# Post-norm decoder layer on one core: tokens transposed by VectorE in 32x32 blocks and regrouped by way of DRAM in place of TensorE's transposes, with self-attention in three streams

## Chip, cores and metric

The kernel runs on one core of a Trainium2 chip, in float32. The metric is the device time of one execution in microseconds (us): the median of several runs. Profiles show one execution; PE is TensorE's matmul, PEld its weight load, DVE is VectorE, ACT is ScalarE, POOL is GpSimd, and SP is SyncE, whose queue (SPq) issues the DMA transfers. L12 means line 12 of the kernel.

## What is computed

One decoder layer over 16 batches of 512 tokens with 256 channels (B = 16, S = 512, C = 256). The reference, cut to its core:

```python
# 1. linear attention: 16 heads of 16 channels, K = 2 states, multiplied
q  = x + x @ Wq + bq
ks = x + x @ Wk[k] + bk[k];  vs = x + x @ Wv[k] + bv[k]        # k = 0, 1
state = prod_k (ks_h.T @ vs_h) / 1024                           # per head, over the 512 tokens
o  = layernorm(q_h @ state) * ln_g + ln_b;  o = o @ Wo + bo
x  = layernorm(x + o)
# 2. cross-attention to 64 context tokens per batch, 16 heads of 64
x  = layernorm(x + softmax(q k.T / 8) v @ Wout.T + b_out)
# 3. 8 experts of 256 -> 1024 -> 256; softmax router; each expert takes
#    the first 1024 tokens whose weight is above 0
x  = layernorm(x + combined expert outputs)
```

## The kernel before

**Tiles.** A batch is NT = 4 tiles of 128 tokens (tokens on partitions, channels along the free axis) and NC = 2 halves of 128 channels. Eight router columns are carried beside the 256 channels, so many tiles are CX = 264 wide. With these inputs the experts take the first two batches (HEAD_B = 2); a loop at the end of the program serves further batches if their tokens have capacity left.

**Work of one batch.** `gram` (L544) multiplies x by itself (ps_g). `self_attention` (L608) loads x again (`load_x`, L603, tile xt), makes the two states (ps_gk L623, ps_s L635), transposes x (`transposed`, L227, into xT), folds the state and Wq into one matrix (ps_m, ps_b), multiplies xT by it (ps_o, L681), normalizes the result z (L687), transposes z (L694) while ScalarE applies gain and shift on the way out of PSUM (zT, L695), multiplies by Wo (ps_p, L705), adds x, normalizes (x1, L713), and transposes x1 (L717) into x1T. A 257th channel row of ones is written into x1T for the mask: VectorE's operation at L237 does it with `not_last`. `cross_attention` (L759) multiplies x1T by keys folded into Wq (ps_sim, L808), makes the softmax (maximum and difference on VectorE, exponential on ScalarE, a product on GpSimd, a 32x32-block transpose on VectorE, L798), and multiplies 128 times with 32 rows each (ps_x, L828). `routing` (L840) normalizes and makes the expert weights. `experts` (L923) is one long run of ps_h (L940) and ps_e (L957) matmuls that has no part in the batches after the first two.

**TensorE's transposes.** `transposed` writes eight 128x128 transposes, four to a PSUM bank; ScalarE and VectorE copy the two banks out. For xT, zT and x1T that is 24 transposes a batch, 384 in all. The weights and the context use the same helper at the start.

**What sets the order.** The parts are Python generators, each in a `Stream` (grams, context, self, cross, routing, experts) with a planned start and span. `weave` (L1004) always resumes the ready stream whose planned time is earliest; `yield` gives up the turn, `yield WAIT` keeps the stream out until the planner's `Model` (L28, durations by engine and size) thinks that its operations are done. `in_order` (L1023) then pins the recorded order on TensorE, VectorE, ScalarE and GpSimd. Nothing is reordered on the chip: an engine that reaches an instruction whose input is late waits, and everything behind it waits too. DMA transfers are all issued by SP in its own order.

**Buffers.** Pool wk1 has one buffer for each name: xt, z, and xT (shared by xT and zT). Pool wk2 has two (x1, x1T, s) and six for the context tiles vo. PSUM has eight banks for everything.

## Time and profile before

| | |
|---|---|
| median of three runs | 1392.32 us (1389.68 to 1394.6) |
| the profiled execution's own time | 1391.12 us |
| its span in the profile | 1389.4 us |
| granted TensorE clock | 0.995 |
| VectorE, ScalarE, GpSimd busy | 850.5, 402.2, 203.9 us |
| DMA moved | 153.57 MB, mean 111 GB/s |
| first ps_x block starts, last one ends | 190.6 us, 1340.4 us |

The profiled execution's time lies 1.7 us above its span and 1.2 us below the median. The page shows busy time by engine, then the span in 40 slices, the DMA queues, the chain of work that ended last, and groups of instructions. A group's mean time is the length of one instruction, but TensorE's instructions overlap; how long one holds the engine is read from the starts in the timeline. TensorE shows two records for each float32 matmul and one for each transpose.

### The profile page before, as it was taken

What the parts mean: (1) busy time and instruction counts of PE and PEld (TensorE: products, weight loads), DVE (VectorE), ACT (ScalarE), POOL (GpSimd) and SP (SyncE); (2) the same over time, 40 slices, a digit from 0 to 9 for tenths busy, and PEclk for the clock granted to TensorE, in tenths of its full rate; (3) what the DMA queues carried; (4) which work ended last, traced back from release to release, by engine and by line L of the source; (5) the groups of instructions that cost most, each with busy time, mean ns of one, the idle gap of its engine ahead of it and who ended that gap; (6) DMA issues with size and microseconds to landing.
All of it is one profiled execution on the core that took longest, in us unless ns stands there. A gap on an engine that the chain in (4) does not pass through costs nothing.

```text
span 1389.4 us, 24206 instructions
## 1 busy us (share of the span) xinstructions
PE 1363.8 (98%) x9630; PEld 1075.8 (77%) x9630; DVE 850.5 (61%) x1957; ACT 402.2 (29%) x912; POOL 203.9 (15%) x140
## 2 busy tenths in 40 slices
PE   7999999999999999999999999999999999999997
PEld 4666676877878787878878787878888787878686
DVE  2345848466583848476584848475675939484744
ACT  1134323132232314142233223142323323232322
POOL 0001112112020111112020112112020202111200
PEclk9999999999999999999999999999999999999999
DMA  8657775511516153421606053513334061505211
GB/s 261 202 121 193 201 188 169 141 32 33 154 46 157 46 141 106 123 80 47 186 18 169 31 141 106 126 62 75 112 94 124 16 187 46 147 26 126 91 55 40
DMA packets 98373, 153.57 MB, mean 111 GB/s; under 512 B 15561, under 2 KB 70097, under 8 KB 98257
## 3 DMA queue, kind: packets, MB, share of 16 engines
q1 hardware_dynamic: 98256, 151.98, 39.9%
q8 instruction: 78, 1.28, 0.4%
q14 instruction: 39, 0.31, 0.1%
HBM read 114.71 MB, written 37.22 MB: 109 GB/s over the span
## 4 chain that ended last, share of the span: by engine, by line
PE 90%; DVE 6%; DMA 2%; ACT 1%; issue 0%; SPq 0%; DVEq 0%; ACTq 0%
PE ps_x L828 17%; PE ps_sim L808 15%; PE ps_e L957 15%; PE ps_h L940 14%; PE ps_p L705 4%; PE ps_gk L623 4%; PE ps_o L681 3%; PE ps_kv L436 3%; PE ps_t L233 2%; PE ps_vo L486 2%; PE ps_kq L745 2%; PE ps_s L635 2%; PE ps_g L549 2%; PE ps_zt L694 1%; PE ps_m L664 1%; PE ps_g L554 1%
## 5 line engine op out<-in xcount | busy, mean ns | idle before, releaser
L940 PE MATMUL ps_h<-head_T,wi 128*128 128x256 f32 x1024 | 239.1, 379 | 0.0
L828 PE MATMUL ps_x<-vo,pT 32*128 32x264 f32 x4096 | 234.4, 385 | 3.7 <-DVE pT L798 3.7
L808 PE MATMUL ps_sim<-kq,x1T 128*128 128x512 f32 x512 | 235.0, 593 | 0.0
L828 PEld LDWEIGHTS ps_x<-vo,pT 32*128 32x128 f32 x4096 | 212.5, 186 | 24.5 <-issue 5.6
L940 PEld LDWEIGHTS ps_h<-head_T,wi 128*128 128x128 f32 x1024 | 193.4, 190 | 38.8 <-issue 13.0
L796 POOL TENSOR_TENSOR s<-s,sm 128x1024 f32<-128x1024 f32 x64 | 121.8, 1903 | 539.1 <-DVE sm L795 500.7
L835 DVE TENSOR_TENSOR x<-ps_x,x 128x264 f32<-128x264 f32 x64 | 23.2, 426 | 225.6 <-PE ps_x L828 225.6
L816 ACT ACTIVATE s<-s 128x512 f32<-128x512 f32 x128 | 80.7, 630 | 276.0 <-DVE s L815 276.0
L808 PEld LDWEIGHTS ps_sim<-kq,x1T 128*128 128x128 f32 x512 | 94.5, 190 | 83.2 <-issue 74.2
L814 DVE TENSOR_REDUCE mx<-ps_sim 128x8 f32<-128x512 f32 x128 | 86.1, 672 | 42.2 <-PE ps_sim L808 41.9
L815 DVE TENSOR_TENSOR s<-ps_sim,mx 128x512 f32<-128x512 f32 x128 | 88.5, 692 | 4.4
L719 POOL TENSOR_TENSOR x<-x,bout 128x1056 f32<-128x1056 f32 x16 | 38.8, 2422 | 320.9 <-ACT hT L946 172.6
L798 DVE STREAM_TRANSPOSE pT<-s 128x1024 f32<-128x1024 f32 x64 | 78.6, 1228 | 7.0 <-POOL s L796 7.0
L946 ACT ACTIVATE hT<-ps_h 128x256 f32<-128x256 f32 x128 | 47.0, 377 | 119.9 <-PE ps_h L940 119.7
L695 ACT ACTIVATE zT<-ps_zt,shift,gain 128x512 f32<-128x512 f32 x32 | 23.2, 776 | 189.7 <-PE ps_zt L694 189.7
L794 DVE TENSOR_REDUCE sm<-s 128x16 f32<-128x1024 f32 x64 | 77.1, 1204 | 0.4 <-ACT s L816 0.4
L267 ACT ACTIVATE x<-x,off,rstd 128x264 f32<-128x264 f32 (+1 forms) x112 | 58.3, 591 | 29.3 <-DVE off L265 29.3
L681 PE MATMUL ps_o<-m,xT 128*128 128x264 f32 x256 | 66.7, 387 | 0.0
L261 ACT ACTIVATE rstd<-bn_mv,eps 128x4 f32<-128x4 f32 (+1 forms) x70 | 20.7, 295 | 158.6 <-DVE bn_mv L250 155.1
L948 DVE TENSOR_SCALAR hT<-ps_h 128x256 f32<-128x256 f32 x128 | 52.1, 409 | 22.5 <-PE ps_h L940 22.3
L705 PE MATMUL ps_p<-wo,zT 128*128 128x264 f32 x256 | 63.1, 387 | 0.0
L436 PE MATMUL ps_kv<-cT,wT 128*128 128x512 f32 x128 | 61.1, 612 | 0.2 <-ACT vst L186 0.2
(172 smaller groups left out, 1892.6 us busy)
## 6 DMA issues: line engine op xcount, KB each, us to landing
vo<-vo_dram SPq DMA_DIRECT2D x512, 132.0 KB, 4.1
vo_dram<-vst SPq DMA_DIRECT2D x128, 132.0 KB, 2.4
xt<-in_x_dram SPq DMA_DIRECT2D x16, 512.0 KB, 4.0
wi<-L_ffn_experts_inter_dram SPq DMA_DIRECT2D x8, 1024.0 KB, 5.1
gx<-in_x_dram SPq DMA_DIRECT2D x15, 512.0 KB, 4.2
x_rest<-x SPq DMA_DIRECT2D x14, 512.0 KB, 3.0
out_dram<-x SPq DMA_DIRECT2D x14, 512.0 KB, 2.9
k_dram<-st SPq DMA_DIRECT2D x16, 256.0 KB, 3.5
```

The source lines that it names most:

```text
L436: nc.tensor.matmul(ps, wT[:, cc, r % 4 * P:(r % 4 + 1) * P], cT[:, cc, q * 512:(q + 1) * 512], start=(cc == 0), stop=(cc == NC - 1),)
L681: nc.tensor.matmul(ps[:, :CX], xT[:, cc, t * P:(t + 1) * P], m[:, cc, :], start=(cc == 0), stop=(cc == NC - 1))
L705: nc.tensor.matmul(ps[:, :CX], zT[:, cc, t * P:(t + 1) * P], wo[:, cc, :], start=(cc == 0), stop=(cc == NC - 1))
L796: nc.gpsimd.tensor_mul(s, s, sm.unsqueeze(2).to_broadcast([P, NH, J]))
L798: nc.vector.transpose(probsT[:, :, t, :], s.rearrange("p h (a j) -> p (h a) j", a=2))
L808: nc.tensor.matmul(ps, x1T[:, cc, t * P:(t + 1) * P], kq[:, cc, hf * 512:(hf + 1) * 512], start=(cc == 0), stop=(cc == NC - 1),)
L814: nc.vector.tensor_reduce(mx[:, hs], sim, AX.X, ALU.max)
L815: nc.vector.tensor_sub(s[:, hs, :], sim, mx[:, hs].unsqueeze(2).to_broadcast([P, 8, J]))
L816: nc.scalar.activation(s[:, hs, :], s[:, hs, :], AF.Exp, scale=SCALE)
L828: nc.tensor.matmul(ps[q][:, :CX], probsT[pq, blk].rearrange("p t i -> p (t i)"), vos[c][pq, i, :], start=(c == 0 and i == 0), stop=(c == 7 ...
L940: nc.tensor.matmul(ps[:, :TB], wi[:, cc, f * P:(f + 1) * P], head_T[b][:, cc, t0 * P:t0 * P + TB], start=(cc == 0), stop=(cc == NC - 1),)
L957: nc.tensor.matmul(ps[:, :C], hT[f][:, t * P:(t + 1) * P], wo_[:, f, :], start=(f == 0), stop=(f == NF - 1),)
```

## The change

The three token transposes of a batch leave TensorE. `to_blocks` lets VectorE transpose each of the four token tiles in 32x32 blocks into one tile xb. `put` writes xb to DRAM with one transfer from ScalarE's queue, and `regroup` reads it back with four transfers of 32 partitions each, in runs of 256 floats, so that channels come to lie on partitions (xT by SP; zT and x1T by ScalarE's queue). xb is a single buffer, and `taken` keeps a second user out until the transfer to DRAM is issued. The transposed tiles now lie as [channel, token tile, half, token], so the matmuls index them as `xT[:, t, cc]`.

For x the blocks are made in `gram`, from gx, and stay in DRAM until `self_attention` loads them; the next gx is loaded after that. Gain and shift, which rode on zT's copy, are folded into Wo and its bias once, at the start: two matmuls and a few VectorE operations in `router_weights`. The ones of x1T are written by ScalarE on a part of x1's blocks (`last_q`). The router columns of z move into xt in 16 small GpSimd copies a batch in place of one.

The states become a stream of their own (`self_states`, `all_states`), and what follows the second normalization (`scores_operand`) another. `yield LIGHT` is a wait after which the stream may be resumed ahead of others, since it issues no TensorE work; `yield HOLD` lets only such streams come between the eight parts of the ps_x block, which stays in one piece on TensorE. The planner takes 0.35 us of ScalarE and 3.0 us to landing for a transfer on ScalarE's queue. Instruction counts, from the order of the two programs: 384 transposes fewer and 2 matmuls more on TensorE; 192 block transposes on VectorE; 176 DMA issues on ScalarE and 64 more on SP.

```diff
+LIGHT = "light"
+HOLD = "hold"
...
+            if kind == "InstDMACopy" and engine == "Activation":
+                start = max(at, self.free.get(engine, 0.0))
+                self.free[engine] = start + 0.35
+                done = start + 3.0
...
+    taken = []
+    def to_blocks(src):
+        while taken:
+            yield LIGHT, 0.5
+        xb = wk1.tile([P, NT, NC, NT, 32], FP, tag="xb", name="xb")
+        for t in range(NT):
+            nc.vector.transpose(
+                xb[:, :, :, t, :].rearrange("p k c j -> p c k j"),
+                src[:, t, :C].rearrange("p (c k j) -> p c k j", c=NC, j=32),
+            )
+        taken.append(xb)
+        yield LIGHT
+        return xb
+    def blocks_dram(name):
+        return dram.tile([NT, 32, NT, NC * NT * 32], FP, tag=name, name=name)
+    def regroup(pool_, tag, name, there, eng):
+        dst = pool_.tile([P, NT, NC, P], FP, tag=tag, name=name)
+        for k in range(NT):
+            eng.dma_start(
+                out=dst[k * 32:(k + 1) * 32].rearrange("i q c n -> i q (c n)"),
+                in_=there[:, :, k, :].rearrange("q i n -> i q n"),
+            )
+        return dst
+    def put(there, xb):
+        nc.scalar.dma_start(
+            out=there.rearrange("q i k n -> (q i) (k n)"), in_=xb.rearrange("p k c t j -> p (k c t j)")
+        )
+        taken.clear()
...
@@ router_columns, router_weights
+            yield WAIT
             ps = bank("ps_rw")
...
+            for dc in range(NC):
+                nc.tensor.matmul(
+                    ps[:, :CX], shift_cols[:, dc, :], wo[:, dc, :], start=(dc == 0), stop=(dc == NC - 1)
+                )
+            nc.vector.tensor_add(cs["bo"], ps[:, :C], cs["bo"])
+            nc.vector.tensor_add(bq_state[:, C:], ps[:, C:CX], bq_state[:, C:])
+            for dc in range(NC):
+                nc.vector.tensor_scalar(wo[:, dc, :], wo[:, dc, :], cs["gain"][:, dc:dc + 1], None, ALU.mult)
...
@@ gram
-            if b + 2 < B:
-                gram_x[b + 2] = load_gram_x(b + 2)
...
+            xb = yield from to_blocks(gx)
+            x_blocks[b] = blocks_dram(f"x_blocks{b}")
+            put(x_blocks[b], xb)
+            if b + 2 < B:
+                gram_x[b + 2] = load_gram_x(b + 2)
...
@@ self_states (was the head of self_attention)
+            yield from until(lambda: finished["self"] >= b, LIGHT)
             state = wk1.tile([P, NC, P], FP, tag="state", name="state")
...
-            yield from until(lambda: made(xt))
-            transposed(xT, xt)
-            yield WAIT
+        def self_attention(b, done):
+            xt = load_x(b)
+            xT = regroup(wk1, "xT", "xT", x_blocks.pop(b), nc.sync)
+            yield from until(lambda: b in states and made(states[b]))
...
-            zT = wk1.tile([P, NC, S], FP, tag="xT", name="zT")
-            for cc in range(NC):
-                ps = bank("ps_zt")
-                for t in range(NT):
-                    nc.tensor.transpose(ps[:, t * P:(t + 1) * P], z[:, t, cc * P:(cc + 1) * P], ident)
-                nc.scalar.activation(
-                    zT[:, cc, :], ps, AF.Identity, bias=cs["shift"][:, cc:cc + 1], scale=cs["gain"][:, cc:cc + 1]
-                )
-            nc.gpsimd.tensor_copy(xt[:, :, C:], z[:, :, C:])
+            for t in range(NT):
+                for q in range(NT):
+                    nc.gpsimd.tensor_copy(xt[q * 32:(q + 1) * 32, t, C:], z[t * 32:(t + 1) * 32, q, C:])
+            zb = yield from to_blocks(z)
+            z_blocks = blocks_dram(f"z_blocks{b % 2}")
+            put(z_blocks, zb)
...
+            yield from until(lambda: made(z_blocks), LIGHT)
+            zT = regroup(wk1, "xT", "zT", z_blocks, nc.scalar)
+            yield
+            yield from until(lambda: made(zT))
...
+            beside(self_st, scores_operand(b, xt, mm))
+        def scores_operand(b, xt, mm):
...
-            transposed(x1T, x1, lambda t: t.rearrange("p (t q i) -> p q t i", q=NT, t=NT), ones=True)
-            yield WAIT
+            x1b = yield from to_blocks(x1)
+            nc.scalar.activation(
+                x1b[:, NT - 1, NC - 1], x1b[:, NT - 1, NC - 1], AF.Identity, bias=last_q[:, 0:1], scale=last_q[:, 1:2]
+            )
+            x1_blocks = blocks_dram(f"x1_blocks{b % 2}")
+            put(x1_blocks, x1b)
+            yield LIGHT, 0.0
+            yield from until(lambda: made(x1_blocks), LIGHT)
+            x1T = regroup(wk2, "x1T", "x1T", x1_blocks, nc.scalar)
+            yield
+            yield from until(lambda: made(x1T))
...
@@ cross_attention, the ps_x block
                 if c < 2:
                     load_vo()
+                if c < 7:
+                    yield HOLD
...
@@ weave
-                st = min(now, key=Stream.time)
+                now = [st for st in now if st.light] or ([held] if held else now)
```

## The prediction

> **What bounds the kernel now.** I read the page's busy line first, then busy time by stage, then the timeline of TensorE around one transpose, then the transfers.
>
> ```profile
> PE 1363.8 (98%) x9630; PEld 1075.8 (77%) x9630; DVE 850.5 (61%) x1957; ACT 402.2 (29%) x912; POOL 203.9 (15%) x140
> PE 90%; DVE 6%; DMA 2%; ACT 1%; issue 0%; SPq 0%; DVEq 0%; ACTq 0%
> ```
>
> TensorE is busy all the time and 90% of the chain that ended last is its own work. Whether that holds in every stage is told by the same count in five stretches (length, then busy time of PE, PEld, DVE, ACT, POOL, clock, DMA share, GB/s): a stretch between two ps_x blocks, a ps_x block, and the start, middle and end of the run.
>
> ```profile
> 665.00:726.00 61.00, 60.87 (x289) 47.78 (x289) 46.65 (x111) 19.05 (x44) 11.96 (x8) 1.00 0.32 95
> 726.00:740.40 14.40, 14.40 (x257) 12.97 (x257) 0.67 (x1) 2.07 (x4) 0.65 (x1) 1.00 0.80 192
> 0.00:190.60 190.60, 178.30 (x881) 115.38 (x881) 96.78 (x227) 58.58 (x134) 17.57 (x27) 0.98 0.70 191
> 190.60:1340.40 1149.80, 1145.10 (x8573) 926.52 (x8572) 727.89 (x1645) 328.29 (x737) 186.35 (x113) 1.00 0.37 100
> 1340.40:1389.40 49.00, 40.41 (x181) 33.88 (x180) 25.81 (x85) 15.38 (x42) 0.00 (x0) 0.97 0.13 42
> ```
>
> In the 1150 us between the first and the last ps_x block TensorE is idle for 4.7 us. The other 20.9 us of idle time lie in the start (12.3) and the tail (8.6). So in the middle every microsecond of TensorE's work taken away is a microsecond gained, as long as no new wait comes. The clock there is 1.00, so there is no throttle to gain from or lose to.
>
> **What a transpose costs.** Its record says 273 ns, but records overlap. The starts in TensorE's timeline tell what eight of them hold:
>
> ```profile
> 699.40 1.04 PE L233 MATMUL ps_t<-ident,xt 128*128 128x128 f32 x8
> 700.27 1.03 PE L940 MATMUL ps_h<-head_T,wi 128*128 128x256 f32 x4
> ...
> 754.43 1.04 PE L233 MATMUL ps_t<-ident,x 128*128 128x128 f32 x8
> 755.30 1.89 PE L957 MATMUL ps_e<-wo__5835,hT 128*128 128x256 f32 x8
> ```
>
> Each group of eight delays the next work by 0.87 us; the zT group, from 740.40 to 741.33, by 0.93. Three groups in 16 batches: 32 x 0.87 + 16 x 0.93 = 42.7 us. Added on TensorE are two 264-wide matmuls at 0.45 us each (ps_p's, 747.50 to 748.39 for two): 0.9 us. **TensorE's work falls by 41.8 us.**
>
> [...]
>
> **What VectorE and ScalarE pay.** VectorE gets 192 block transposes of 256 elements. Before has only the four times larger one:
>
> ```profile
> L798 DVE STREAM_TRANSPOSE pT<-s 128x1024 f32<-128x1024 f32 x64 | 78.6, 1228 | 7.0 <-POOL s L796 7.0
> ```
>
> A quarter of 1228 ns is 0.31 us, the lower end; a 512-element VectorE pass (L815) takes 0.69, the upper end. I take 0.35, near the quarter because the time of the larger one follows its length: 67 us (59 to 133). The copies of xT and x1T leave VectorE: 16 x (0.683 + 0.810) = 24 us. Net 43 us, or 2.7 a batch. Between two ps_x blocks VectorE is 46.65 of 61 us busy, 76%; with all of it there and 2.6 us less TensorE work, 49.3 of 58.4, 84%. In the ps_x block it is idle but for 0.67 us, and the light streams may use that. I cost it at nothing, covered by this idle time. ScalarE loses 32 x 0.776 + 9.4 + 9.2 = 43 us and gains 16 copies of 128 elements (0.25 each, 4 us) and 176 DMA issues. An issue on SP takes 0.39 us (xt's row, below); on ScalarE none is shown. I bound it by nothing and by 0.63, one of its exponentials (L816), and take SP's 0.39: 69 us. ScalarE is at 29%: hidden, except that each issue holds evacuations behind it, four in a row for 1.6 us, in which TensorE fills about four of eight banks (ps_h, 0.43 us a bank).
>
> **What the path of a token tile pays.** This is what can cost time: TensorE's order is fixed, so a late xT, zT or x1T stops it. The nearest rows are the loads of xt (512 KB, runs of 1024 bytes, like a regrouping), the first fence, and the stores of x2_rest (512 KB, like a put), the second. The SPq row has min, median and max of one issue in ns.
>
> ```profile
> L605 SPq DMA_DIRECT2D xt<-in_x_dram x16: 389/390/556, 38.3 to 1208.0; - x16
> ...
> DMA to landing us min/median/max: 3.8/4.0/5.7
> ```
>
> ```profile
> L864 SPq DMA_DIRECT2D x_rest<-x x14: 383/384/400, 376.7 to 1347.4; - x14
> ...
> DMA to landing us min/median/max: 2.8/3.0/4.5
> ```
>
> From the last ps_o to a loaded zT: sum, statistics and normalization of one tile 2.55 us (in the tail of the timeline, 1379.54 to 1382.09), three more tiles 1.5, four block transposes 1.4, the put 0.4 + 3.0, four issues 1.2 and the last landing 4.0: **14 us**; x1T has the same and a copy of 0.25. With the maxima it is 17.5. I counted the TensorE work between the two ends in the changed kernel's order, with the issue times of before's timeline (0.86 us for a 512-wide matmul, 0.43 for 256, 14.45 for a ps_x block). From last ps_o to first ps_p it is 19.2 us at the least in 16 batches, with a median near 28; from last ps_p to first ps_sim 19.1 at the least, with a median near 28. In the order of before the smallest are 10.5 and 7.2. So all 32 paths have 1.6 us or more over the slow sum.
>
> xT has its blocks in DRAM long before, but shares its buffer with zT, so its load waits for the last ps_p of the batch before. There the next ps_o follows after 3.2 us in the third batch, then 7.4 or more in all others. The load needs 1.2 + 4.0 = 5.2: **2 us** lost once. SP waits for that buffer too, and vo, xt and weight transfers stand behind it; the same happens before with xt, also a single buffer, and vo is needed some 60 us later.
>
> DMA moves 48 x 0.52 MB out and as much in: 153.6 MB become 204, and its share of 40% grows by bytes to about 53%. It is at 0.80 during ps_x, where the vo loads of the next batch run, so puts and loads that fall there come near their maxima, which the covers still hold.
>
> GpSimd's 16 small copies a batch, at 0.21 us each by the one copy that they replace (L698), and the sum behind them (2.36, L699) take 5.7 us and must end before the first ps_p's sum; they run beside the 10 us of put and load, and cost 0, or at worst the 3.2 us by which they grew if a softmax product (1.9 us) stands ahead.
>
> The DMA semaphores and single buffers add waits that no row shows: ScalarE now waits for puts before it issues loads. In the order a regrouping often stands directly behind its put, so ScalarE stands for some 3 us. Between nothing (it has nothing else ready) and 1 us for each of 32, I take 4 us in all, near the lower end since ps_x or VectorE's evacuations cover most of them.
>
> The start: a wait of 3.3 us (ps_rw for VectorE, L376) is given its own place in the plan; the two for pT ahead of ps_x, 3.7 together, are unchanged. Against it, gx is reloaded later, after its block transposes. I take these as equal, between 4 us less and 10 more, as idle time in the start is 12.3.
>
> **Sum.** 1389.4 - 41.8 + 2 + 4 = 1353.6 span; with the 1.7 us outside the span **1355 us**, 2.7% below the median of 1392.3 and 36 below the profiled execution's 1391.1. Taken without any new wait it is 1351, with 4 us less at the start 1347.
>
> **Rivals.**
>
> Better packing (0.18): the longer covers also take away waits that busy time hides in the start, where ps_g takes 0.41 us a record against 0.22 in the middle. With some 10 us of them gone it is 1340 to 1347. For it: 20.9 of 25.6 us idle lie outside the middle. Against: the start waits for input transfers.
>
> VectorE becomes the bound (0.17): at 84% between ps_x blocks its queue runs late, and TensorE waits for banks. At 1 to 2 us in each of 16 batches it gives 1365 to 1385. For it: 0.69 us for a transpose would add 5.5 us a batch, not 2.7. Against: ps_x leaves 13.7 us idle.
>
> Transfers eat the gain (0.08), slower than before: put and load behind the vo burst. If the path takes 26 us instead of 14, the sum of what is missing over the 32 counted covers is 39 us, so the gain is gone; at 28 it is 64 and the run takes 1355 + 64 = 1419 us. For it: a vo load of only 132 KB lands in 4.1 us in the median (page, DMA issues), so there is a backlog in the burst. Against it: 26 us need each of the two landings near 9 to 10 us, and the maxima shown are 4.5 and 5.7.
>
> That the change does not take the work off TensorE is excluded: the order has 384 transposes fewer.
>
> **How the numbers follow.** Forecast 0.55 (1347 to 1362), better packing 0.18, VectorE 0.17, transfers 0.08, and 0.02 near no change. The range takes in the first three but the ends: 1340 to 1380, leaving out 0.08 + 0.02 and some of the tails. A difference of 0.3%, 4 us, is about what a measurement of this kernel can tell. Faster 0.89 (the first three, less the far end of the third), same 0.03, slower 0.08.
>
> **What will show it.** ps_t and ps_zt rows gone except for weights, context and the head (106 transposes left); TensorE busy near 1322 us; idle in the middle under 15 us. Block transposes near 0.35 us each. Waits of ps_o, ps_p and ps_sim for transfers a few us in all; if they hold over 20 us, the covers were misjudged. If waits for VectorE after ps_sim or ps_h hold 20 us, the second rival is right. ScalarE's DMA issues at 0.4 us; if they take 1 us or more, ScalarE holds the banks and the forecast falls.

## The result and the profile after

The changed kernel takes **1462.88 us** (median of four runs, 1459.41 to 1467.07) against 1392.29 for the kernel before on the same chip: ratio 1.0509, 95% interval 1.047 to 1.0548. It is slower by 71 us where 37 us less than this median were forecast. The profiled execution has a span of 1457.7 us and a mean granted clock of 0.969 (before 1389.4 and 0.995). Further down, one of e3's four executions took 3585 us and is left out of its median.

The page of the changed kernel, busy time, then busy tenths of TensorE, its granted clock and DMA in 40 slices, then the chain that ended last:

```profile
PE 1363.8 (94%) x9250; PEld 1054.4 (72%) x9250; DVE 880.0 (60%) x2123; ACT 369.2 (25%) x864; POOL 247.9 (17%) x380
...
PE   7797998799899999999999999999999998999897
...
PEclk9899999899999999999999999999999999999999
DMA  8717869533451717463364527352727264533521
...
PE 56%; DVE 20%; DMA 7%; ACT 3%; issue 2%; SPq 1%; ACTq 0%; POOL 0%; DVEq 0%; POOLq 0%
```

TensorE has 380 instructions less and the same busy time, and its own work is 56% of the chain instead of 90%. The missing digits lie in the first third. Three of the prediction's stretches (up to the first ps_x, from there to the last one's end, the tail; length, then busy time of PE, PEld, DVE, ACT, POOL, clock, DMA share, GB/s) are now:

```profile
0.00:223.10 223.10, 192.99 (x883) 125.22 (x883) 108.21 (x270) 55.59 (x128) 23.10 (x56) 0.92 0.68 189
223.10:1404.80 1181.70, 1125.47 (x8165) 890.73 (x8164) 744.05 (x1764) 297.17 (x690) 224.76 (x324) 0.98 0.49 135
1404.80:1457.70 52.90, 45.32 (x204) 38.50 (x204) 27.76 (x90) 16.47 (x46) 0.00 (x0) 0.96 0.11 39
```

The start became 32.5 us longer, and the middle, which should have lost some 40 us of work, is 32 us longer. Idle time in the middle is 56.2 us (before 4.7). What TensorE waited for (us in total, times, longest):

```profile
PE ps_sim L880 <- DMA x1T<-x_blocks: 13.9, 3, 5.5
PE ps_rw L416 <- DVE early L412: 9.1, 1, 9.1
PE ps_o L739 <- DMA xT<-x_blocks: 8.5, 2, 6.3
PE ps_vo L535 <- ACT vst L193: 7.1, 6, 6.1
PE ps_s L684 <- DVE gk L673: 6.8, 1, 6.8
PE ps_e L1034 <- DVE hT L1025: 5.8, 4, 3.8
```

No single row explains the 109 us that are accounted for below; there are few waits for the transposed tiles themselves and many for VectorE and ScalarE.

**Why idle time is only part of it.** TensorE's timeline around the longest wait for x1T (start, length, operation), then three neighbouring stretches around the same place:

```profile
432.53 1.89 PE L1017 MATMUL ps_h<-head_T,wi 128*128 128x256 f32 x8
439.91 8.88 PE L880 MATMUL ps_sim<-kq,x1T 128*128 128x512 f32 x16 [5.49 <-DMA x1T<-x_blocks]
448.63 1.03 PE L1017 MATMUL ps_h<-head_T,wi 128*128 128x256 f32 x4
```

```profile
429.00:436.70 7.70, 5.42 (x25) 4.39 (x24) 4.85 (x17) 2.84 (x7) 0.00 (x0) 1.00 0.73 235
436.70:443.50 6.80, 3.59 (x5) 1.55 (x6) 0.00 (x0) 0.00 (x0) 0.00 (x0) 0.50 0.51 123
443.50:450.00 6.50, 6.50 (x20) 3.46 (x19) 5.28 (x8) 1.89 (x3) 0.00 (x0) 1.00 0.00 0
```

Sixteen ps_sim records take 8.72 us up to the next start, where eight products at 0.86 need 6.9: for 6.8 us the granted clock is 0.50, 3.2 of them still within the stall. So the stall of 5.5 us cost 1.8 us more in slow work. The changed kernel has 16 such half-clock stretches, 91.2 us together, the kernel before four, 15.4 us. TensorE was busy in 62.8 and 10.2 us of them; half of the difference, **26 us**, is lost work time. It is most of why busy time did not fall by 41 us. The account of the span: work 41 us less, idle time 68 more (93.9 against 25.6), half clock 26 more, 15 not assigned (perhaps short gaps that the records' overlap hides): 68 us more.

**The path of one tile.** The chain of waits from 425 to 442 us in the changed kernel (start, length, what):

```profile
425.37 5.67 DMA x_blocks<-xb
431.04 0.02 issue
431.06 0.32 ACTq L267
...
432.52 7.26 DMA x1T<-x_blocks
439.78 0.14 issue
439.91 2.90 PE ps_sim L880 x3
```

From the put to the loaded x1T are 14.4 us, where the prediction took 8.6 (11.8 with the maxima). In that time a store of 512 KB (x_rest, issued 424.72) and a load of 1024 KB (wo_, issued 430.97) are under way, and the DMA engines are busy for 0.90 of the put and 0.99 of the load (the last but one figure of each line):

```profile
425.40:431.00 5.60, 5.60 (x28) 4.88 (x27) 4.80 (x19) 0.73 (x3) 0.28 (x1) 1.00 0.90 323
432.50:439.80 7.30, 1.92 (x9) 1.33 (x8) 1.52 (x5) 2.34 (x5) 0.00 (x0) 0.79 0.99 274
```

A single piece of x1T lands in 3.1 us in the median, 7.4 at worst, but a tile needs its put and the last of four pieces. Where the trace tells all these landings, the way from the put's issue to the loaded tile takes 12.8 us in the median for x1T (6 batches, 7.3 to 14.1) and 10.8 for zT (7 batches, 7.1 to 11.9). So the 8.6 us were too little in general, and not in one bad place alone.

What stands ahead of the put grew more. From the last ps_p to the put of x1 the prediction counted 5.7 us (sum, statistics, normalization, block transposes, copy); the changed kernel's trace has 10.6 at the least and 15.0 in the median of the 16 batches. In the kernel before, the last ps_p to the first transpose of x1 took 5.0 to 8.9 us. The whole way of x1, from the last ps_p to the loaded tile, is 21.5 to 42.2 us in those 6 batches, 24.6 in the median, where the prediction has 14 (17.5 with the maxima). Some of this is the planner's choice, which may place other work ahead where the cover is long; how much is not shown.

**A common measure.** To compare kernels whose orders differ, every TensorE instruction is priced by its issue time in the kernel before, as in the prediction (0.86 us for a 512-wide product, 0.43 for 256, 0.87 for eight transposes, so 0.109 for one), and the sum in program order is taken from the start of the same instruction in the trace. What is left is time lost to waits and half clock up to there. In us:

| kernel | TensorE work | lost at first ps_x of batch 1 | 5 | 9 | lost at the end | from 9 to end |
|---|---|---|---|---|---|---|
| before | 1332.9 | 33 | 42 | 44 | 50 | 6 |
| after | 1291.9 | 62 | 104 | 123 | 159 | 36 |

109 us more lost, 41 saved. 62 of the 109 are lost before the fifth batch's ps_x, the rest a few us in every batch.

### The profile page after: what moved, and what is told of

It is laid out like the page before. It is cut to its first block, busy times and chain, and to the rows that moved or that the text cites. A ratio compares the mean times of both kernels' runs of the same rounds, so it can differ in the third digit from the quotient of the medians.

```text
span 1457.7 us, 24199 instructions
## 1 busy us (share of the span) xinstructions
PE 1363.8 (94%) x9250; PEld 1054.4 (72%) x9250; DVE 880.0 (60%) x2123; ACT 369.2 (25%) x864; POOL 247.9 (17%) x380
## 3 DMA queue, kind: packets, MB, share of 16 engines
q8 instruction: 75, 1.23, 0.4%
## 4 chain that ended last, share of the span: by engine, by line
PE 56%; DVE 20%; DMA 7%; ACT 3%; issue 2%; SPq 1%; ACTq 0%; POOL 0%; DVEq 0%; POOLq 0%
PE ps_x L900 15%; PE ps_sim L880 10%; PE ps_e L1034 10%; PE ps_h L1017 9%; DVE sm L866 3%; PE ps_p L765 2%; DVE bn_st L285 2%; DMA x_blocks<-xb 2%; DVE s L887 2%; PE ps_gk L672 2%; DVE mx L886 2%; DVE pT L870 2%; DMA vo<-vo_dram 2%; PE ps_o L739 2%; PE ps_kq L817 2%
## 5 line engine op out<-in xcount | busy, mean ns | idle before, releaser
L880 PE MATMUL ps_sim<-kq,x1T 128*128 128x512 f32 x512 | 237.4, 608 | 13.9 <-DMA x1T<-x_blocks 13.9
L900 PE MATMUL ps_x<-vo,pT 32*128 32x264 f32 x4096 | 242.5, 387 | 3.2 <-DMA vo<-vo_dram 1.9
L900 PEld LDWEIGHTS ps_x<-vo,pT 32*128 32x128 f32 x4096 | 215.8, 187 | 27.2 <-DMA vo<-vo_dram 4.0
L880 PEld LDWEIGHTS ps_sim<-kq,x1T 128*128 128x128 f32 x512 | 99.2, 196 | 115.8 <-issue 109.7
L739 PEld LDWEIGHTS ps_o<-m,xT 128*128 128x128 f32 x256 | 49.2, 195 | 22.9 <-issue 12.4
L303 ACT ACTIVATE x<-x,off,rstd 128x264 f32<-128x264 f32 (+1 forms) x112 | 58.3, 592 | 23.9 <-DVE off L301 14.1
L751 POOL COPY xt<-z 32x8 f32<-32x8 f32 x256 | 47.2, 184 | 97.3 <-DVE z L742 88.2
```

What stands on the lines that cost most here:

```text
L739: nc.tensor.matmul(ps[:, :CX], xT[:, t, cc], m[:, cc, :], start=(cc == 0), stop=(cc == NC - 1))
L880: nc.tensor.matmul(ps, x1T[:, t, cc], kq[:, cc, hf * 512:(hf + 1) * 512], start=(cc == 0), stop=(cc == NC - 1),)
L900: nc.tensor.matmul(ps[q][:, :CX], probsT[pq, blk].rearrange("p t i -> p (t i)"), vos[c][pq, i, :], start=(c == 0 and i == 0), stop=(c == 7 ...
```

## The experiments

Theories: (1) the plan gives a transfer too little time to land; (2) the single block buffer makes VectorE stand; (3) ScalarE, standing at its DMA issues, holds its other work; (4) rival: the new streams cost it, not the way through DRAM. Every edit makes the planner write a new order, so single waits move; the table of lost time behind h2 is the common measure, and a difference of a few us between two such orders is not put down to the edit.

**e1: a longer landing in the plan.**

```diff
-                done = start + 3.0
+                done = start + 7.0
```

> The same kernel, with one number of the plan changed: a transfer issued by ScalarE is planned to land 7.0 us after its start instead of 3.0, so the streams move the products that read zT and x1T further away. Theory 1, the plan places the readers too close to the transfers (zT and x1T pieces land in 2.6 us at best, 3.1 in the median and 6.8 to 7.4 at worst in the trace of the changed kernel): the waits of ps_sim and ps_p for x1T and zT (13.9 us in all) go, with the half-clock stretches behind them, and the time falls by 20 to 30 us, to 1432 to 1443. If the single buffer of the block transposes or ScalarE's own queue is the cause, it stays within 8 us of 1463, and the waits of ps_s and ps_h for VectorE and ScalarE are as before.

Measured: 1466.07 us, 1.0549 (1.0524 to 1.0575). ps_sim no longer waits for x1T, yet nothing is gained; TensorE now waits elsewhere:

```profile
PE ps_x L900 <- DMA vo<-vo_dram: 12.0, 10, 4.0
```

Theory 1 falls as the main cause: with this plan the delay is moved, not removed.

**e2: two block buffers.**

```diff
-        while taken:
+        while len(taken) > 1:
-... tag="xb", name="xb")
+... tag="xb", name="xb", bufs=2)
-        taken.clear()
+        taken.pop(0)
-        dst = pool_.tile([P, NT, NC, P], FP, tag=tag, name=name)
+        dst = pool_.tile([P, NT, NC, P], FP, tag=tag, name=name, bufs=1)
```

> Two buffers for the transposed blocks instead of one, so that VectorE does not stand until the transfer of the tile before has landed. To make room x1T has one buffer instead of two (its load is issued 12 us of TensorE work or more after the last product that read the one before, so this should cost nothing). Theory 2, VectorE standing at the block buffer (26.6 us of its waits in the changed kernel, one of which held TensorE for 6.9 us) is the main loss: 1435 to 1448. If it is the landing of transfers or ScalarE's queue: 1455 to 1465, with VectorE's wait for the block buffer near zero all the same.

Measured: 1429.67 us, 1.0286 (1.0261 to 1.0311): **33 us** less, for a second block buffer of 4 KB a partition (x1T has one buffer instead of two to make room, and the order is a new one). This row of VectorE's waits in the changed kernel is gone:

```profile
DVE xb L253 <- DMA x_blocks<-xb: 26.6, 8, 6.6
```

VectorE stood 26.6 us for the tile before to land, and all its other work, in order behind that, stood with it. e5 below repeats the gain with the other landing (29 us less than e1). Theory 2 holds for a third of the 109 us; 38 us above the kernel before remain.

**e3: SP issues the transfers.**

```diff
-        nc.scalar.dma_start(out=there...
+        nc.sync.dma_start(out=there...
-zT = regroup(..., nc.scalar)     x1T = regroup(..., nc.scalar)
+zT = regroup(..., nc.sync)       x1T = regroup(..., nc.sync)
```

> The three transfers out and the loads of zT and x1T are issued by SP instead of ScalarE. Theory 3, it is ScalarE, standing at its DMA issues (DMA waits of 89.9 and 34.0 us ahead of hT and s) and so late with evacuations and normalizations: 1425 to 1445, and the waits of TensorE for ScalarE (ps_vo 7.1, ps_e 4.8, ps_h 3.3 us) halve. Against it: SP's queue is in order and holds the vo, xt and weight loads, and a wait for a tile stands ahead of them; if transfers behind each other are the loss wherever they are issued, it is 1460 to 1500, with vo later and new waits ahead of ps_x.

Measured: 1469.52 us, 1.0561 (1.0532 to 1.0591). Not better. TensorE's waits for ScalarE's vst and hT fell a little (in ps_vo from 7.1 to 4.2 us, in ps_e from 4.8 to 3.9), but its waits for x1T and zT grew to 29.4 and 24.2 us (13.9 and none in the changed kernel). So the stand moves to another queue, and what ScalarE's costs is not settled: theory 3 is not confirmed.

**e4: the three streams, all transposes on TensorE.** xT, zT and x1T are made as before; xt is loaded only when x1 of the batch before is normalized, since TensorE's order would otherwise wait for itself.

> The three streams and the new order of the changed kernel, but xT, zT and x1T made on TensorE as in the kernel before, and no blocks in DRAM: TensorE has all its 41.8 us of transposes again. If the way through DRAM is the whole loss, this is as fast as the kernel before or a little faster, 1380 to 1400, with the clock near 0.99. If the streams and their new order cost it (rival), it is 1450 or more, with idle time and half-clock stretches like those of the changed kernel.

Measured: 1415.76 us, 1.0175 (1.0152 to 1.0198), between the two theories. With the same TensorE work as before the new order loses 24 us. In its profiled execution, which is 12.8 us above its median, 11.5 us are waits for xt. So the order costs something by itself, most of it before the fifth batch, and the way through DRAM costs 47 us more in spite of 42 us less work.

**e5: e2 and e1 together.**

> Two block buffers (with one x1T buffer) and the planned landing of 7.0 us together. With two buffers alone (1429.7 us) ps_sim still waited 15.5 us for x1T in four places and ps_o 5.3 us for xT, with half-clock stretches behind them; with the landing of 7.0 alone x1T was never late, but ps_x waited 12.0 us for vo in ten places. If the late x1T is the rest of the loss in the middle: 1400 to 1412. If the longer plan only turns these waits into waits for vo (rival): 1425 to 1440, with 8 us or more of waits of ps_x for vo.

Measured: 1437.56 us, 1.0298 (1.0259 to 1.0338), with 8.5 us of waits of ps_x for vo. The rival holds: waits are traded.

**e6, e8: one part undone, in the new streams.** In e6 x stays on TensorE (xt loaded as in e4), z and x1 go through DRAM; in e8 only x goes through DRAM.

> Only z and x1 go through DRAM; xT is made on TensorE from xt (14 us of transposes again), so the block buffer has two users a batch instead of three, and the first batches' blocks and xT loads are gone from the start. xt must now be there before ps_o. If the three users of the one block buffer and the xT loads are the loss: 1425 to 1440 (33 us of the block buffer and 15 of xT less, 14 of transposes more). If z and x1, which are on the path, are the loss: 1455 to 1480.

> The three streams of the changed kernel, only x through DRAM, zT and x1T on TensorE. Against the kernel with all three on TensorE in these streams (1415.8 us, where TensorE waited 11.5 us for xt): 14 us of work and the waits for xt less, 1385 to 1398, if x through DRAM is harmless and the streams are not. If the streams themselves cost about 20 us against the old order, this is 15 to 25 us above the same transport in the old order.

Measured: e6 1419.75 us, 1.0182 (1.0131 to 1.0233); e8 1421.83 us, 1.0195 (1.0175 to 1.0215). Each takes 41 to 43 us off although it gives TensorE 14 or 28 us of work back. In both the waits of VectorE for a block's landing, 26.6 us in the changed kernel, are gone, so part of this is what e2 gained; the two were not run with a second buffer. e6 is below both of its expectations, e8 some 24 us above the one without a cost of the streams.

**e7, f1, f3, f7: x alone, in the order of before.** The single self-attention stream is kept; only x's blocks go through DRAM (with a planned landing of 7.0 us, and the 16 small GpSimd copies).

```diff
+            xb = yield from to_blocks(gx)        # in gram
+            x_blocks[b] = blocks_dram(f"x_blocks{b}")
+            put(x_blocks[b], xb)
-            transposed(xT, xt)                   # in self_attention
+            xT = regroup(wk1, "xT", "xT", x_blocks.pop(b), nc.sync)
```

> The kernel before with its one self-attention stream and its order, and only x through DRAM: blocks made from gx after the gram product, some 200 us ahead of their use, xT loaded by SP (the selected weights share w_all, as in the changed kernel, to make room). zT and x1T stay on TensorE. If a way through DRAM costs nothing where it has time (theory): 14 us of TensorE work less, 1374 to 1386. If the loads of xT and the puts disturb vo, xt and the weights even so (rival): 1392 to 1410.

Measured: 1447.63 us, 1.0381 (1.036 to 1.0402), far from both. One row tells why:

```profile
PE ps_m L694 <- DVE state L690: 36.4, 16, 4.0
```

The transposes of xt had stood between VectorE's state product and ps_m and covered it; taking them away laid 2.3 us bare in each batch. f1 adds a pause in the plan (`yield WAIT` before ps_m), f3 has it and starts with the fifth batch, f7 with the ninth:

```diff
+            yield WAIT                                  # f1, f3, f7
+            if b >= QB:   # f3 (4);  f7: if b >= 8
                 xb = yield from to_blocks(gx)
```

> As x alone in the old order (1447.6 us), with one pause more in the plan, between VectorE's state product and ps_m. In that run ps_m waited for the state in all 16 batches, 36.4 us in all: the transposes of xt on TensorE had stood there and covered it. If that uncovered wait is why x alone in the old order lost 53 us: 36 us of waits and some 10 us of half clock go, 1395 to 1405. If the transfers of x themselves are the loss: 1425 or more.

> The same with the pause, but the first four batches keep their transposes of xt on TensorE, so that the start, where DMA was at 0.70 to 0.79 in the kernel before, has no blocks to carry. 12 batches give 10.4 us of TensorE work back. If the start is where x through DRAM costs: 1380 to 1388, below the kernel before. If it costs in the middle as well (VectorE, xT behind zT in one buffer): 1392 to 1400.

> The old order, x through DRAM only from the ninth batch on, so that the order and the traffic of the first 350 us are nearly those of the kernel before; 8 batches give 7.0 us of TensorE work back. In the run from the fifth batch on (1398 us) TensorE was at work all the time after 360 us, but had lost some 17 us more than the kernel before up to there. If way and cover are the whole matter, and x costs nothing in the middle: 1384 to 1388, a little faster than before. If the middle does lose something that the busy time hides: 1391 to 1396.

Measured: f1 1408.84 us, 1.0117 (1.0084 to 1.015); f3 1398.35 us, 1.0044 (1.0029 to 1.0058); **f7 1386.76 us, 0.9957 (0.9944 to 0.997), faster than both kernels**. Lost time at the fifth batch's ps_x: 73, 60 and 44 us, before 42. f1 lies 4 us above its first range, and f3 in the range that its expectation gave to a cost in the middle; yet f3 loses hardly more than before from the fifth batch on (9 us against 8), so the loss lies ahead of that. x costs where its blocks fall in the first 350 us, and next to nothing later: f7 gains 5.7 us by the medians (3.8 by the profiled spans) of the 7.0 that 8 groups of transposes hold. No run has f7's other edits alone, but the table below speaks for the work as the cause: it is 7.0 us less, and the lost time 3 us more. The middle of f7:

```profile
449.00:1340.00 891.00, 890.04 (x6552) 715.36 (x6551) 573.94 (x1332) 257.04 (x577) 178.49 (x255) 1.00 0.39 107
```

TensorE is idle for 1.0 of 891 us. There, for x, the price of a transpose, and that VectorE's block transposes are hidden, stand as predicted.

**f5, f10, f11: two buffers, and the way through DRAM only later.** In f5 x goes through DRAM from the fifth batch on, z and x1 in all; in f10 all three tiles from the ninth on; f11 is f10 with a planned landing of 5.0.

> The changed kernel with two block buffers (1429.7 us), and xT of the first four batches on TensorE. In the two-buffer run TensorE was busy 94.8 and 99.0 of the first 112 and second 112 us at a clock of 0.94 and 0.92, against 101.5 and 109.7 at 0.97 and 1.00 before. If the blocks of x in the start cause most of that: 1400 to 1412 (15 to 25 us less, 3.5 us more transposes). If the new streams are late in the start for other reasons (zT and x1T of the first batches beside the context): 1420 to 1432.

> The changed kernel with two block buffers (1429.7 us), all three tiles of the first eight batches transposed on TensorE (21 us of its work again), and through DRAM from the ninth batch on. If the loss lies in the start, where context, vo and weights are written and loaded: 1395 to 1412. If it lies in every batch alike (x1T late behind its 3.0 us of plan): 1420 to 1435.

> The same with a planned landing of 5.0 us for ScalarE's transfers, between 3.0 (x1T late in four places) and 7.0 (vo late in nine). If the late x1T is what each batch still loses: 8 to 15 us less than with 3.0. If any plan only trades one wait for another: within 5 us of it.

Measured: f5 1439.28 us, 1.0356 (1.0307 to 1.0406), above both of its ranges and slower than e2: its start loses 15 us less up to the fifth batch, and its middle 24 more, with x1T late in five places. f10 1424.43 us, 1.0222 (1.0201 to 1.0243); f11 1424.09 us, 1.0226 (1.0196 to 1.0255). From the ninth batch on f10 and f11 lose 31 and 32 us, before 6. So the middle does lose with all three tiles, with a planned landing of 3.0 and of 5.0 (in f11 x1T is never late).

**g3, g1: do the queues, or xT and zT, hold each other?** The program orders show that SP's and ScalarE's transfers rotate over the same eight completion semaphores, as all 176 of ScalarE's do in the changed kernel's trace. g3 is e2 with `nc.gpsimd` in place of `nc.scalar` for put and regroup; g1 gives xT a tile of its own (`"xTx"` for `"xT"`; x1T has one buffer).

> Two block buffers (1429.7 us), and all transfers that ScalarE issued (the blocks out, zT and x1T in) issued by GpSimd. In the changed kernel the transfers of SP and ScalarE take turns on the same 8 completion semaphores: 64 of ScalarE's 176 issues wait for the end of an unrelated transfer of SP first, and 58 of SP's for one of ScalarE; GpSimd's have 8 of their own. If this sharing is what makes ScalarE stand (20 to 28 us at a time for vo) and SP late: 1400 to 1415, no wait of ScalarE for vo, and less than half of TensorE's waits for hT. If the transfers' own time or the order is the rest: 1422 to 1435. If GpSimd's issues hold the softmax products behind them: above 1435.

> The changed kernel, xT in a buffer of its own instead of sharing zT's (x1T has one buffer instead of two, to make room), so that SP can load xT a batch ahead and does not stand with the vo and xt loads behind it. If the shared buffer is the loss (ps_o waited 8.5 us for xT, SP 142 us for zT in front of it): 1435 to 1448, no wait of ps_o for xT. If SP stands for zT's completion semaphore and not for the buffer: within 8 us of 1463, with SP's waits for zT still there.

Measured: g3 1493.11 us, 1.0727 (1.0698 to 1.0756). ScalarE no longer stands for vo, but TensorE waits more, GpSimd itself stands for the puts of x1 to land, and an issue on GpSimd is dearer (ns, min, median, max; then the landing of x1T):

```profile
PE ps_sim L880 <- DMA x1T<-x_blocks: 60.3, 8, 9.8
POOL x1T L267 <- DMA x_blocks<-xb: 55.1, 12, 7.4
```

```profile
L267 POOL DMA_DIRECT2D x1T<-x_blocks x64: 550/552/580, 147.1 to 1396.5; - x64
DMA to landing us min/median/max: 2.8/4.2/7.5
```

On ScalarE's queue in the changed kernel the same loads have 443 ns and 3.1 us in the median. So ScalarE's waits for vo (89.9 us ahead of hT and 34.0 ahead of s in the changed kernel) go with its issues, but to part the queues this way costs more than it gives; whether the sharing matters by itself stays open. g1 1456.06 us, 1.0446 (1.0406 to 1.0487): the wait of ps_o for xT is gone, and with it SP's wait for zT. The gain is 7 us by the medians, 1 us by the profiled spans, and the intervals of the two ratios overlap: at most 7 us.

**h1, h2: z or x1?** Both are f10 with one tile more on TensorE in all batches, z in h1, x1 in h2.

```diff
-            yield WAIT if b < 8 else LIGHT
-            if b < 8:
+            yield WAIT if b < B else LIGHT
+            if b < B:                       # h1: at z's places; h2: at x1's
```

> As the run in which all three tiles go through DRAM from the ninth batch on (1424.4 us), but z stays on TensorE in all batches; x and x1 go through DRAM from the ninth on. That run lost 31 us between the first ps_x of the ninth batch and the end, against 8 to 10 with all three on TensorE or x alone through DRAM in the same streams, and saved 7.0 us of TensorE work for each tile. If x1, which has the scores behind it, is what costs: as much lost, and 7 us less saved, 1428 to 1434. If it is z, with the loads of xT behind its own: lost 10 to 15, 1412 to 1418.

> The same with x1 on TensorE in all batches; x and z go through DRAM from the ninth on. If x1 is what costs, the loss from the ninth batch on falls from 31 to 10 to 15 us: 1412 to 1418. If it is z: 1428 to 1434. If each costs half, both runs are near 1422.

Measured: h1 1434.45 us, 1.0292 (1.0245 to 1.0339); h2 1405.44 us, 1.0107 (1.0082 to 1.0132). **Of the two, it is x1 that costs.** h1 and h2, 760 to 1400 us:

```profile
760.00:1400.00 640.00, 620.86 (x4570) 493.28 (x4569) 396.17 (x933) 166.78 (x388) 121.50 (x165) 0.99 0.41 116
```

```profile
760.00:1400.00 640.00, 634.56 (x4675) 512.23 (x4673) 412.09 (x990) 172.59 (x409) 117.22 (x163) 1.00 0.41 117
```

Same DMA, 19.1 against 5.4 us of idle time. In h1 x1T is never late itself; TensorE waits for hT instead (760 to 1420 us):

```profile
PE ps_e L1070 <- ACT hT L1059: 7.2, 5, 3.8
PE ps_e L1070 <- DVE hT L1061: 4.6, 3, 4.0
```

One such place in h1, first TensorE, then VectorE:

```profile
1064.01 3.19 PE L1070 MATMUL ps_e<-wo__8615,hT 128*128 128x256 f32 x14
1070.95 1.16 PE L1070 MATMUL ps_e<-wo__8615,hT 128*128 128x256 f32 x2 [3.76 <-ACT hT L1059]
```

```profile
1064.33 0.69 DVE L923 TENSOR_TENSOR s<-ps_sim,mx 128x512 f32<-128x512 f32 x1
1064.94 1.21 DVE L902 TENSOR_REDUCE sm<-s 128x16 f32<-128x1024 f32 x1
1066.18 0.25 DVE L903 RECIPROCAL sm<-sm 128x16 f32<-128x16 f32 x1
1066.35 0.78 DVE L691 SCALAR_TENSOR_TENSOR gk<-bk_row,u,ps_gk 128x256 f32<-128x256 f32 x2
1067.05 1.48 DVE L317 SCALAR_TENSOR_TENSOR off<-bn_mv,rstd 128x4 f32<-128x4 f32 x1
1068.54 1.25 DVE L906 STREAM_TRANSPOSE pT<-s 128x1024 f32<-128x1024 f32 x1
```

VectorE's rows leave no pause here, though this `off` is recorded with 1.48 us where 0.15 is the median in h1; what held it is not shown. ScalarE waits for it before z's normalization (1068.56), and hT, behind that in ScalarE's order, comes at 1070.54.

The table, all kernels (lost time in us as above):

| kernel | through DRAM | work | batch 1 | 5 | 9 | end | 9 to end | median us |
|---|---|---|---|---|---|---|---|---|
| before | none | 1332.9 | 33 | 42 | 44 | 50 | 6 | 1392.3 |
| after | x, z, x1 | 1291.9 | 62 | 104 | 123 | 159 | 36 | 1462.9 |
| e1 | x, z, x1 | 1291.9 | 66 | 94 | 123 | 153 | 30 | 1466.1 |
| e2 | x, z, x1 | 1291.9 | 59 | 93 | 102 | 124 | 22 | 1429.7 |
| e3 | x, z, x1 | 1291.9 | 52 | 96 | 125 | 173 | 48 | 1469.5 |
| e5 | x, z, x1 | 1291.9 | 66 | 89 | 102 | 137 | 35 | 1437.6 |
| f5 | z, x1; x from 5th | 1295.4 | 51 | 78 | 95 | 133 | 38 | 1439.3 |
| g1 | x, z, x1 | 1291.9 | 62 | 98 | 119 | 158 | 39 | 1456.1 |
| g3 | x, z, x1 | 1291.9 | 57 | 96 | 131 | 189 | 58 | 1493.1 |
| e6 | z, x1 | 1305.9 | 48 | 66 | 78 | 102 | 24 | 1419.7 |
| f10 | all from 9th | 1312.9 | 44 | 67 | 72 | 103 | 31 | 1424.4 |
| f11 | all from 9th | 1312.9 | 42 | 66 | 74 | 106 | 32 | 1424.1 |
| h1 | x, x1 from 9th | 1319.8 | 45 | 66 | 73 | 108 | 35 | 1434.5 |
| h2 | x, z from 9th | 1319.8 | 41 | 64 | 68 | 76 | 8 | 1405.4 |
| e8 | x | 1319.8 | 59 | 81 | 84 | 94 | 10 | 1421.8 |
| e4 | none | 1333.8 | 52 | 69 | 78 | 86 | 8 | 1415.8 |
| f1 | x, old order | 1318.9 | 53 | 73 | 75 | 83 | 8 | 1408.8 |
| f3 | x from 5th, old | 1322.4 | 35 | 60 | 62 | 69 | 7 | 1398.4 |
| f7 | x from 9th, old | 1325.9 | 35 | 44 | 46 | 53 | 7 | 1386.8 |
| e7 | x, old, no pause | 1318.9 | 48 | 82 | 93 | 120 | 27 | 1447.6 |

(e4's profiled execution took 1428.6 us, 12.8 above its median, so its losses may be up to 13 us high.) The column before the last parts the kernels: with x1 through DRAM 22 to 58 us, without it 6 to 10, e7 with its bare state product apart. x and z together save 14 us of TensorE work in 8 batches and lose 2 more than before.

The column of the fifth batch parts the start. f10, f11, h1 and h2 have the new streams and move no block through DRAM before the ninth batch: 64 to 67 us, against 42 before. So the new order alone accounts for 22 to 25 of the 62 us that the changed kernel loses there. e6, with z and x1 through DRAM from the first batch on, stands at 66 as well. So what comes on top in the start comes with x's blocks, alone (e8 81; in the old order f1 73) or with the others (after 104).

## Why the prediction was wrong, step by step

The price of the work was right. The term that failed is the sum's "+ 2 + 4" for new waits: 109 us were lost in their place, 68 of them idle time, 26 half clock, 15 not assigned. The prediction's own sign for misjudged covers, over 20 us of waits of ps_o, ps_p and ps_sim for transfers, came true with 8.5 + 13.9 us and shows only a fifth of this.

- **Work off TensorE, 41.8 us**: right in price. f7 shows it where no wait comes, for x alone: 5.7 us measured for 7.0 counted.
- **"The clock there is 1.00, so there is no throttle to gain from or lose to"**: wrong. The mean clock of that middle was 1.00 with 4.7 us of idle time in it; at the new stalls it was 0.50 for a while, as for 6.8 us at the 5.5 us wait for x1T. 26 of the 109 us are this. A sign of it was there: in the kernel before the clock is 0.50 from 31.2 to 34.6 us, behind a stall of 3.3, and ps_g's records start 0.43 us apart there and 0.22 later. The rival of better packing takes such slow ps_g records for hidden waits.
- **VectorE's transposes**: 0.40 us each (taken 0.35), net 53 us. Hidden in f7. The second rival, VectorE as the bound, is no general one (60% busy), but in h1 VectorE's rows leave no pause from 1055 to 1071 us, around the place shown. In before a batch's scores (ps_sim) are spread over some 26 us in the median; in the kernels with the new streams over 20 to 23. The rows for a batch's softmax on VectorE add up to 21.6 us (4 x (2 x 0.67 + 2 x 0.69 + 1.20 + 0.25 + 1.23)), so "at 84% between ps_x blocks" was a mean over a stretch with this burst in it. But the burst alone does not explain the loss: VectorE is busy for 86% of it in before and 81% in the changed kernel, and h2, e4 and e8, which lose 8 to 10 us from the ninth batch on, have nearly the same spread as h1 (22 us). ScalarE's issues took 0.34 us for a put and 0.44 for a load in the median, as predicted, and ScalarE is 25% busy.
- **"So all 32 paths have 1.6 us or more over the slow sum"**: the step that failed in the middle. The way of 14 us (17.5) was mis-sized: for x1 it took 24.6 us in the median of the batches that can be read, and no less than 21.5. From put to load it is 12.8, not 8.6 and at most 11.8, as landings grew to 7.5 and 7.4 us; ahead of the put it is 15.0 (all batches), not 5.7. I counted each step by its own length and left out what else VectorE and ScalarE have to do in between. But late tiles are not the whole: planned away (e1, f11) or not, x1 through DRAM loses some 3 us a batch and saves 0.9.
- **Single buffers and semaphores, "4 us in all"**: the mis-sized term. A second block buffer is worth 33 us (e2). I weighed ScalarE's waits, and not VectorE's, which stands for a landing that it need not know of, with all evacuations behind it.
- **xT behind zT, 2 us**: 8.5 us of waits in the changed kernel; removing them gains at most 7 (g1).
- **The start, "I take these as equal", between 4 us less and 10 more**: 62 us lost up to the fifth batch. The order alone loses 22 to 25 (f10, f11, h1, h2; e4 27, which may be high), the block buffer 11 (e2), and x alone 31 in the old order (f1). These overlap and are not a sum. One mechanism is visible: VectorE's copy of `st` waits up to 8.0 us for k_dram's store, and ps_rw 9.1 for VectorE behind it (3.3 before). It need not be the blocks' traffic: in f10, which moves none there, such a copy waits 8.0 us as well, only that ps_rw does not stand behind it. By what way x's blocks cost time in the start is not settled.
- **Rivals**: "transfers eat the gain" had the right sign and 0.08; the path of 26 us that it priced came near (24.6 in the median for x1). But it put this down to landings of 9 to 10 us, which were 7.5 at most, and TensorE's waits for x1T and zT hold 13.9 us, not 39 to 64: late tiles are not the main cost. "Better packing" did not come: idle time in the start grew from 12.3 to 30.1 us.

Not settled: why x1 costs, and z, which has the same hops, does not. x1 has the scores, and so VectorE's burst, right behind it; that it pushes the burst into other work is what h1's lines show in one place, not a proof. A rival is untested: with its transport x1 also gets another place in the planner's order (`LIGHT` in place of `WAIT`), and no run has that order with x1 on TensorE. z through DRAM in the old order, and x1 as the only tile through DRAM, were not run.

## What to carry to other kernels

Work taken off a saturated engine is only worth its price where nothing takes its place: put the new way first where TensorE is dense and the traffic low (here x from the ninth batch, 0.4% faster), and see what the removed work had covered (36 us of bare waits in e7). Give the source of an asynchronous transfer more than one buffer (here a second one was worth 33 us), since an engine that stands for a landing holds all its other work (VectorE stood 26.6 us so), and price a stall of TensorE with the half clock that came with it here (at all 65 stalls over 4 us in the table below, usually 3.4 to 10.2 us of it). A path is not free because the bound engine has enough work beside it: count as well what the engines that carry it have to do at that moment, not in the mean.

## What the runs showed of the hardware

**Behind a longer stall of TensorE its granted clock is 0.50 for a while.** Stalls in the profiles of all 20 kernels, where no other idle time over 0.7 us in all lay within 14 us ahead or 7.5 behind:

| stall, us | stalls | with half clock behind | its usual length, us |
|---|---|---|---|
| 0.5 to 1 | 76 | 2 | 3.4 |
| 1 to 1.5 | 64 | 13 | 3.4 |
| 1.5 to 2 | 41 | 12 | 3.4 |
| 2 to 2.5 | 27 | 15 | 3.4 |
| 2.5 to 3.5 | 31 | 26 | 3.4 |
| 3.5 to 4 | 12 | 10 | 3.4 or 6.8 |
| 4 to 5 | 20 | 20 | 3.4 or 6.8 |
| 5 to 7 | 24 | 24 | 6.8 |
| over 7 | 21 | 21 | 10.2 or 6.8 |

Part of the slow stretch lies within the stall itself, so the longest wait for x1T, 5.5 us, cost 1.8 more, and in the changed kernel 68 us of added idle time brought 26 more in slow work. In the kernel before and the changed kernel 18 of the 20 half-clock stretches are 3.4, 6.8 or 10.2 us long. No single length of stall parts the rows: 2 of 76 stalls under 1 us have half clock behind them, 15 of 27 from 2 to 2.5 us, and all 65 over 4 us.

A 32x32 block transpose on VectorE, 128x256 elements in float32, took 0.402 us and 128x1024 took 1.23: by an estimate from these two, some 0.13 us and 1.08 ns for each element along the free axis. Landing times in the changed kernel spread widely: 512 KB written in 2.6 to 7.5 us, 128 KB read in 2.6 to 7.4.
